# Decoder kernel on one core: the attention's values product moved behind the next step's scores, half of a copy given to GpSimd in the last block, and the first values products placed between the first scores

## The chip, the core and the metric

The kernel runs on one core of a Trainium2 chip. A core has five engines, each with its own instruction stream: TensorE (PE, matrix products; its weight loads are listed as PEld), VectorE (DVE), ScalarE (ACT), GpSimd (POOL) and SyncE (SP, which here only issues DMA transfers). They work from SBUF, the on-chip memory of 128 partitions; PE writes its results to PSUM, from which DVE and ACT read them. [...]

The metric is the time of one execution on the device in microseconds (us). A profiled execution of the same kernel, with a start and a length for each instruction, stands beside it.

## The reference

The input `x` has 8 sequences of 256 tokens with 256 features. Three parts follow one another, each with a residual and a layer norm:

```python
x = layernorm(x + attention(x))        # causal, 16 heads of 64
x = layernorm(x + cross_attention(x))  # 3 rounds against 120 context rows, each with a GRU cell
x = layernorm(x + ffn(x))              # shared MLP + best 2 of 8 experts
```

The change concerns the first part, and in a small place the beginning of the second:

```python
q, k, v = x @ Wq, x @ Wk, x @ Wv                       # 1024 columns: 16 heads of 64
logits = einsum('nhid,nhjd->nhij', q, k) / 8 + causal
out = einsum('nhij,nhjd->nhid', softmax(logits), v)
return out @ Wo + bo
```

All of it is computed in float32.

## The kernel before

The 2048 tokens are taken in four blocks of 512, which is two sequences each (`NBLK`, `BLK`, `BPB`). The attention runs in 64 steps; a step is one block `i`, one pair of heads `pr` and one sequence `bi` of the block, so there are 16 steps to a block. For a step:

- `scores` (L313) makes the products of queries and keys on PE for both heads, lower triangle only: for each head a 128x128 tile and a 128x256 tile, 384 columns together, in the PSUM tiles `pp` (a ring of three banks, two used by a step).
- `least` (L328) adds the mask on DVE and takes each row's minimum of the negated scores (four instructions with `nmax` as a second result); then ACT makes the exponentials in four instructions with their row sums, `sums`.
- `weigh` (L358) takes the reciprocal of the sums on DVE, and GpSimd multiplies the tile `sc` by it in two instructions.
- `split` (L370) separates the high and the low 16 bits of the float32 weights into `planes`: ACT copies all 1536 halves in one instruction. Then SP issues a DMA transpose of 16-bit words to `turned`.
- `joined` (L382) puts the two halves together again on DVE, which gives `pT`, the transposed weights.
- `attend_values` (L391) multiplies values by `pT` on PE, in `po`, and copies the result to `OT`: on ACT in blocks 0 to 2, on DVE in the last block.

`planes`, `turned`, `pT` and `po` have two buffers each, `sc` has four.

Beside the steps runs work of other blocks: `project` (L292) makes the queries or keys of the pair two or three ahead (PE, then a DVE copy `qk`); `values` (L303) makes an eighth of the next block's values; `outputs` (L415) multiplies a finished block by `Wo` and adds it to `X`; `to_feature_major` transposes a block on PE; `between` (L422) spreads these over the 16 steps of a block at fixed places (`V_AT`, `O_AT`), and near a block's end also takes the root for the layer norm (`root`, ACT and DVE) and scales the rows (`scaled`, DVE). `context_normed` puts small works of the second part into blocks 1 and 2, among them GpSimd products at L197.

In this part the order on PE, ACT, DVE and GpSimd is the order of the program text (`manual_schedule`, L257 and L262), so the driver loop (L485 to L501) is the schedule. The main loop takes step `k` to its end while step `k + 3` (`ahead` is 3) gets its scores and `k + 2` is weighed and split. SP's queue is in program order too: first the loads of the weights, then one transpose per step.

After the steps the remaining outputs are made, PSUM is taken over by new pools, and the second part begins with `context_transposed` (four groups of PE transposes, copied to `pnT` by DVE), `weights_joined` (two products `pa`, copied to `AT`, and two groups `pc`, copied to `C`) and `keys`, which needs both (L1003 to L1005). There DVE's and GpSimd's order comes from the planner; PE's and ACT's is still that of the text.

Of the kernel before, what the change touches and what calls it, by code (L numbers as in the profile page):

```python
# [12 lines left out]
U16 = mybir.dt.uint16  # L13
# [4 lines left out]
B, S, D = 8, 256, 256  # L18
# [7 lines left out]
NBLK = NT // BLK  # L26
NSUB = BLK // P
BPB = BLK // S
NPAIR = H // 2
# [32 lines left out]
def decoder_kernel(  # L62
# [23 lines left out]
    nc = tc.nc  # L86
# [14 lines left out]
    def evac(dst, src):  # L101

        flip[0] ^= 1
        if flip[0]:
            nc.vector.tensor_copy(dst, src)
        else:
            nc.scalar.copy(dst, src)
# [150 lines left out]
    with (  # L258
# [29 lines left out]
        OT = [None] * NBLK  # L288
# [3 lines left out]
        def project(g, which):  # L292

            i, pr = divmod(g, NPAIR)
            w = (wq_sb, wk_sb)[which]
            pq = bank(f"pq_{g}_{which}")
            for dc in range(DC):
                nc.tensor.matmul(pq, w[:, dc, ts(pr, P)], XT[i][:, dc, :], start=dc == 0, stop=dc == DC - 1)
            t = a4.tile([P, BLK], F32, tag=f"qk{which}", name=f"qk_{g}_{which}")
            nc.vector.tensor_copy(t, pq)  # L300
            qk[g, which] = t

        def values(i, n, hf):  # L303
            if V[i] is None:
                V[i] = a2.tile([P, NSUB, H * HD], F32, tag="v", name=f"v_{i}")
            pv = bank(f"pv_{i}_{n}_{hf}")
            for dc in range(DC):
                nc.tensor.matmul(
                    pv, XT[i][:, dc, ts(n, P)], wv_sb[:, dc, ts(hf, 512)], start=dc == 0, stop=dc == DC - 1
                )  # L310
            nc.vector.tensor_copy(V[i][:, n, ts(hf, 512)], pv)

        def scores(k):  # L313
            i, pr, bi = steps[k]
            g = i * NPAIR + pr
            qT, kT = qk[g, 0], qk[g, 1]
            t0 = bi * S
            pp = [ps_s.tile([P, 512], F32, tag="pp", name=f"pp_{k}_{h}") for h in range(2)]
            rows2 = [slice(h * HD, (h + 1) * HD) for h in range(2)]
            for h, r in enumerate(rows2):  # L320
                nc.tensor.matmul(pp[h][:, 0:P], qT[r, ds(t0, P)], kT[r, ds(t0, P)], start=True, stop=True)
            for h, r in enumerate(rows2):
                nc.tensor.matmul(pp[h][:, P:384], qT[r, ds(t0 + P, P)], kT[r, ds(t0, S)], start=True, stop=True)  # L323
            live[k] = pp
# [3 lines left out]
        def least(k):  # L328

            pp = live.pop(k)  # L330
            sc = a4.tile([P, 2, 384], F32, tag="sc", name=f"sc_{k}")
            nmax = stat.tile([P, 2, 2], F32, tag="nmax", name="nmax")
            for h in range(2):
                for t in range(2):
                    nc.vector.tensor_tensor_reduce(  # L335
                        out=sc[:, h, seg[t]],
                        in0=pp[h][:, seg[t]],
                        in1=mask[:, seg[t]],
                        scale=-(HD**-0.5),
                        scalar=3.0e38,  # L340
                        op0=ALU.add,
                        op1=ALU.min,
                        accum_out=nmax[:, t, h : h + 1],
                    )
            sums = stat.tile([P, 2, 2], F32, tag="sums", name="sums")
            for h in range(2):
                for t in range(2):
                    nc.scalar.activation(  # L348
                        sc[:, h, seg[t]],
                        sc[:, h, seg[t]],  # L350
                        AF.Exp,
                        scale=-1.0,
                        bias=nmax[:, t, h : h + 1],
                        accum_out=sums[:, t, h : h + 1],
                    )
            live[k] = sc, sums
# [13 lines left out]
        def split(k):  # L370

            sc, sums = live.pop(k)
            n = 2 * 384
            planes = a2.tile([P, 2, n], U16, tag="planes", name=f"planes_{k}")
            nc.scalar.copy(planes, sc.rearrange("p h c -> p (h c)").bitcast(U16).rearrange("p (n w) -> p w n", w=2))  # L377
            turned = a2.tile([P, 2 * n // P, P], U16, tag="turned", name=f"turned_{k}")
            nc.sync.dma_start_transpose(turned, planes.rearrange("p w n -> p (w n)"))
            live[k] = turned  # L380

        def joined(k):  # L382
            turned = live.pop(k)
            pT = a2.tile([P, 2, 384], F32, tag="pT", name=f"pT_{k}")
            nc.vector.tensor_copy(  # L385
                pT.rearrange("p h c -> p (h c)").bitcast(U16).rearrange("p (n w) -> p w n", w=2),
                turned.rearrange("p (w c) q -> p w (c q)", w=2),
            )
            live[k] = pT

        def attend_values(k):  # L391
            i, pr, bi = steps[k]
            pT = live.pop(k)
            if OT[i] is None:
                OT[i] = a2.tile([P, NPAIR, BLK], F32, tag="ot", name=f"ot_{i}")
            po = ps_o.tile([P, 512], F32, tag="po", name=f"po_{k}")[:, 0:S]
            for c, q0 in ((0, 0), (1, P)):
                for h in range(2):
                    nc.tensor.matmul(  # L399
                        po[ts(h, HD), q0:S],  # L400
                        V[i][:, 2 * bi + c, ts(2 * pr + h, HD)],
                        pT[:, h, 0:S] if c == 0 else pT[:, h, S:384],
                        start=c == 0,
                        stop=c == 1,
                    )
            if i + 1 < NBLK:
                nc.scalar.copy(OT[i][:, pr, ts(bi, S)], po)
            else:
                nc.vector.tensor_copy(OT[i][:, pr, ts(bi, S)], po)

        def add_bo(i):

# [2 lines left out]
        def outputs(i, n):  # L415
            py = bank(f"py_{i}_{n}")[:, 0:D]
            for pr in range(NPAIR):
                nc.tensor.matmul(py, OT[i][:, pr, ts(n, P)], wo_sb[:, pr, :], start=pr == 0, stop=pr == NPAIR - 1)
            nc.vector.tensor_tensor(X[i][:, n, :], py, X[i][:, n, :], ALU.add)
            MV[i] = moments(X[i], MV.get(i), (n,))  # L420
# [25 lines left out]
        ahead = 3  # L446
# [18 lines left out]
        add_bo(0)  # L465
        for which in range(2):
            project(0, which)
        for k in range(2):
            scores(k)
            least(k)  # L470
        weigh(0)
        values(0, 0, 0)
        split(0)
        values(0, 0, 1)
        weigh(1)
        split(1)
        for which in range(2):
            project(1, which)
        scores(2)
        least(2)  # L480
        for n in range(1, NSUB):
            for hf in range(2):
                values(0, n, hf)
        project(2, 0)
        for k in range(len(steps)):  # L485
            i, j = divmod(k, 2 * NPAIR)
            if k + ahead - 1 < len(steps):
                weigh(k + ahead - 1)
            if k + ahead < len(steps):
                scores(k + ahead)  # L490
                least(k + ahead)
            if k + ahead - 1 < len(steps):
                split(k + ahead - 1)
            joined(k)
            if k + 5 < 2 * NBLK * NPAIR:
                project(*divmod(k + 5, 2))
            elif k >= len(steps) - NSUB:

                outputs(NBLK - 2, k - len(steps) + NSUB)
            between(i, j)  # L500
            attend_values(k)  # L501
        normalize(X[NBLK - 2], MV[NBLK - 2])
        for n in range(NSUB):
            outputs(NBLK - 1, n)
# [118 lines left out]
                    ALU.mult,  # L623
                )

    def weights_joined():
        for d in range(DC):
            pa = bank(f"pa_{d}")
            for o in range(DC):
                nc.tensor.matmul(pa[:, 0:D], xwk_sb[:, o, ts(d, P)], xwq_sb[:, o, :], start=o == 0, stop=o == DC - 1)  # L630
            evac(AT[:, d, :], pa[:, 0:D])
        for d in range(DC):
            pc = big(f"pc_{d}")
            for hf in range(2):
                for o in range(DC):
                    nc.tensor.matmul(
                        pc[:, hf, 0:384],
                        xwv_sb[:, o, ts(d, P)],
                        wih_sb[:, o, ts(hf, 384)],
                        start=o == 0,  # L640
                        stop=o == DC - 1,
                    )
            evac(C[:, d, :].rearrange("p (a b) -> p a b", a=2), pc[:, :, 0:384])
# [352 lines left out]
    def both(*fs):  # L996
# [3 lines left out]

        return f

    context_transposed()  # L1003
    weights_joined()
    keys()  # L1005
    for p in range(2):
        norms(p)
# [265 lines left out]
    for a in range(half):  # L1273
        n = half + a
# [69 lines left out]
```

## Time and profile before

| | us |
|---|---|
| median of three runs (1064.96 to 1066.25) | 1065.13 |
| profiled execution | 1096.06 |
| its span, first to last instruction | 1094.4 |

The columns of the next table are stretches of the trace in us from its start, and busy us of each engine in that stretch.

| stretch | what runs | length | PE | DVE | ACT | POOL |
|---|---|---|---|---|---|---|
| 0 to 35.7 | loads, first projections and values | 35.7 | 32.3 | 13.3 | 10.3 | 6.9 |
| 35.7 to 112.4 | block 0 | 76.7 | 72.2 | 52.8 | 56.6 | 28.3 |
| 112.4 to 203.5 | block 1 | 91.1 | 88.3 | 59.0 | 63.0 | 31.9 |
| 203.5 to 288.4 | block 2 | 84.9 | 82.1 | 54.3 | 54.7 | 30.4 |
| 288.4 to 339.4 | block 3, steps with a projection | 51.0 | 44.5 | 39.5 | 39.4 | 19.4 |
| 339.4 to 376.4 | last steps and outputs | 37.0 | 34.5 | 18.8 | 8.9 | 6.9 |
| 376.4 to 736 | second part, shared MLP's first half, routing | 359.6 | 346.4 | 171.0 | 151.6 | 82.7 |
| 736 to 1094 | experts and end | 358.0 | 339.6 | 61.3 | 91.6 | 30.9 |

A busy PE is not a PE at its peak, since matmuls overlap and their ends are modelled; a gap in PE's row is a real gap, however. The granted TensorE clock is full but for five dips to half: at 198 us for 3.4 us, at 676 and 707 for 6.8 each, at 1041 for 17, and from 1092 on. The costliest groups of the attention steps by the page, with the number of instructions, total and mean: ACT's exponentials (L348) x256, 113.3 us, 444 ns; GpSimd's weighing (L363) x128, 105.4 us, 845 ns; ACT's `planes` (L377) x64, 93.2 us, 1457 ns; DVE's minima (L335) x256, 76.3 us, 354 ns; DVE's `pT` (L385) x64, 70.0 us, 1094 ns.

### The profile page before, as it was taken

The page shows a single profiled execution, that of the slowest core. Times are in us where ns is not written, and L with a number is a line of the kernel's source. Part 1 is how long each engine was busy: PE and PEld are TensorE (multiplying, and loading weights), DVE is VectorE, ACT ScalarE, POOL GpSimd, SP SyncE. Part 2 cuts the span into 40 slices and gives each one's busy share as a digit, 9 for nine tenths or more (in the row PEclk, how much of TensorE's full clock was granted, in tenths as well). Part 3 has the DMA queues.
Part 4 walks back from the last instruction along what each step waited for, and adds up shares of the span by engine and source line. Part 5 has one row for each costly group of instructions (what it writes and reads, how often), then busy time and mean ns, then how long its engine had stood idle before and what let it go on. Part 6 is the DMA issues. An engine that isn't in the chain of part 4 may idle for free. (4 is left out here: it accounts for less than half of the span.)

```text
span 1094.4 us, 13674 instructions
## 1 busy us (share of the span) xinstructions
PE 1039.8 (95%) x4686; PEld 720.9 (66%) x4686; DVE 470.0 (43%) x1394; ACT 476.0 (43%) x1140; POOL 237.3 (22%) x264
## 2 busy tenths in 40 slices
PE   8999999999888999999999999699999999999967
PEld 5444555555445755556565668588888888888756
DVE  3666666666776542434443687300011010110137
ACT  3567776666776024555555443122222222222213
POOL 2333422532234211221211023500000000000550
PEclk9999999999999999999999998999999999999969
DMA  9634433433344499940000011246675667663231
GB/s 325 107 76 84 86 65 67 73 73 71 74 87 94 153 348 348 349 140 0 1 1 1 0 40 39 78 155 219 205 249 204 232 203 248 215 211 111 82 97 62
DMA packets 195492, 144.24 MB, mean 132 GB/s; under 512 B 107551, under 2 KB 185951, under 8 KB 195423
## 3 DMA queue, kind: packets, MB, share of 16 engines
q1 hardware_dynamic: 191263, 132.88, 42.2%
q0 software_dynamic: 3072, 8.39, 2.4%
q10 hardware_dynamic: 1088, 2.10, 0.5%
q8 instruction: 37, 0.61, 0.2%
q14 instruction: 32, 0.26, 0.1%
HBM read 72.70 MB, written 45.48 MB: 108 GB/s over the span
## 5 line engine op out<-in xcount | busy, mean ns | idle before, releaser
L1053 ACT ACTIVATE hT_t<-ph_t,bt 128x256 f32<-128x256 f32 (+1 forms) x184 | 71.3, 438 | 202.6 <-issue 154.6
L363 POOL TENSOR_TENSOR sc<-sc,sums 128x256 f32<-128x256 f32 (+1 forms) x128 | 105.4, 845 | 212.5 <-DVE sums L360 212.5
L348 ACT ACTIVATE sc<-sc,nmax 128x128 f32<-128x128 f32 (+1 forms) x256 | 113.3, 444 | 72.5 <-DVE nmax L335 72.5
L1044 PE MATMUL ph_t<-xgT,w 128*128 128x256 f32 (+1 forms) x736 | 140.3, 348 | 0.8 <-ACT hT_t L1053 0.8
L1058 PE MATMUL pf_t<-w,hT_t 128*128 128x256 f32 x624 | 138.3, 379 | 0.0
L739 PE MATMUL gate<-XT,whh_sb 128*128 128x512 f32 x288 | 133.8, 593 | 0.0
L1044 PEld LDWEIGHTS ph_t<-xgT,w 128*128 128x128 f32 x736 | 123.8, 190 | 15.0 <-ACT hT_t L1053 1.0
L1058 PEld LDWEIGHTS pf_t<-w,hT_t 128*128 128x128 f32 x624 | 116.9, 190 | 15.0
L1172 POOL DMA_INDIRECT y<-yd,slot x32 | 30.9, 967 | 323.7 <-PE ph_s L1044 309.2
L335 DVE CUSTOM_DVE_ANT_0 sc<-pp,mask 128x128 f32<-128x128 f32 (+1 forms) x256 | 76.3, 354 | 52.3 <-PE pp L323 50.7
L377 ACT COPY planes<-sc 128x1536 uint16<-128x1536 uint16 x64 | 93.2, 1457 | 8.5 <-POOL sc L363 8.5
L739 PEld LDWEIGHTS gate<-XT,whh_sb 128*128 128x128 f32 x288 | 54.3, 190 | 48.5 <-issue 46.2
L1044 PE MATMUL ph_s<-XT,sh 128*128 128x256 f32 x256 | 66.6, 415 | 20.2 <-issue 19.3
L399 PEld LDWEIGHTS po<-pT,v 128*64 128x64 f32 x512 | 32.9, 136 | 68.1 <-issue 25.4
L1044 PEld LDWEIGHTS ph_s<-XT,sh 128*128 128x128 f32 x256 | 53.1, 210 | 32.1 <-issue 22.6
L748 PEld LDWEIGHTS gate<-at,G 120*128 120x128 f32 x288 | 54.5, 189 | 29.9 <-issue 23.3
L399 PE MATMUL po<-pT,v 128*64 128x256 f32 (+1 forms) x512 | 55.7, 337 | 19.1 <-DVE pT L385 15.0
L748 PE MATMUL gate<-at,G 120*128 120x256 f32 x288 | 72.1, 379 | 0.4 <-DVE at L598 0.4
L1149 DVE COPY xgT<-xg 128x512 f32<-128x512 f32 (+1 forms) x23 | 14.0, 611 | 131.8 <-PE xg L1147 131.8
L385 DVE COPY pT<-turned 128x1536 uint16<-128x1536 uint16 x64 | 70.0, 1094 | 0.0
L598 DVE TENSOR_TENSOR yo<-pf_t,b2t 128x512 f32<-128x512 f32 (+1 forms) x23 | 14.0, 610 | 127.9 <-PE pf_t L1058 127.9
L1053 ACT ACTIVATE hT_s<-ph_s,vec_sb 128x256 f32<-128x256 f32 x64 | 26.9, 471 | 90.5 <-PE ph_s L1044 44.6
(208 smaller groups left out, 1479.6 us busy)
## 6 DMA issues: line engine op xcount, KB each, us to landing
w<-in_ew_dram SPq DMA_DIRECT2D x46, 1024.0 KB, 5.5
xd<-zeros SPq DMA_DIRECT2D x1, 16640.0 KB, 51.3
yd<-zeros SPq DMA_DIRECT2D x1, 16640.0 KB, 99.4
xg<-xd SPq DMA_DIRECT2D x16, 256.0 KB, 5.3
yd<-yo SPq DMA_DIRECT2D x16, 256.0 KB, 5.6
b2t<-in_b_dram SPq DMA_DIRECT2D x23, 128.0 KB, 5.2
sh<-in_sh_w_dram SPq DMA_DIRECT2D x2, 1024.0 KB, 6.9
X<-in_x_dram SPq DMA_DIRECT2D x3, 512.0 KB, 11.7
```

Source lines behind the costliest of these rows:

```text
L335: nc.vector.tensor_tensor_reduce(out=sc[:, h, seg[t]], in0=pp[h][:, seg[t]], in1=mask[:, seg[t]], scale=-(HD**-0.5), scalar=3.0e38, op0=AL ...
L348: nc.scalar.activation(sc[:, h, seg[t]], sc[:, h, seg[t]], AF.Exp, scale=-1.0, bias=nmax[:, t, h : h + 1], accum_out=sums[:, t, h : h + 1],)
L363: nc.gpsimd.tensor_tensor(sc[:, :, seg[t]], sc[:, :, seg[t]], sums[:, t, :].unsqueeze(2).to_broadcast([P, 2, w]), ALU.mult,)
L377: nc.scalar.copy(planes, sc.rearrange("p h c -> p (h c)").bitcast(U16).rearrange("p (n w) -> p w n", w=2))
L385: nc.vector.tensor_copy(pT.rearrange("p h c -> p (h c)").bitcast(U16).rearrange("p (n w) -> p w n", w=2), turned.rearrange("p (w c) q -> p ...
L399: nc.tensor.matmul(po[ts(h, HD), q0:S], V[i][:, 2 * bi + c, ts(2 * pr + h, HD)], pT[:, h, 0:S] if c == 0 else pT[:, h, S:384], start=c == ...
L739: nc.tensor.matmul(pg[:, oc, :], whh_sb[:, dc, o], XT[i][:, dc, :], start=dc == 0, stop=not given and dc == DC - 1,)
L748: nc.tensor.matmul(pg[:, oc, ts(bi, S)], G[:, BPB * i + bi, o], AT_[p][:, bi, :], start=not hidden, stop=not hidden or bi == BPB - 1,)
L1044: nc.tensor.matmul(ph[:, a, 0:w], w1_sb[:, dc, ts(c, P)], rhs[:, dc, :], start=dc == 0, stop=dc == DC - 1,)
L1053: nc.scalar.activation(hT[:, c, 0:w], ph[:, a, 0:w], AF.Gelu_apprx_tanh, bias=bias[:, c : c + 1])
L1058: nc.tensor.matmul(po, hT[:, c, ts(a, P)], w2_sb[:, c, :], start=c == 0, stop=c == FC - 1)
L1172: nc.gpsimd.indirect_dma_start(out=y, out_offset=None, in_=yd[:, :], in_offset=bass.IndirectOffsetOnAxis(ap=slot[:, g : g + 1], axis=0),)
```

## The change

Four edits:

1. In the driver loop `attend_values` is called one turn later and at another place: for step `k - 1`, after the scores and minima of step `k + 3` and before `split`. The loop gets one more turn at its end. The last outputs of block 2 (`outputs(NBLK - 2, ...)`) go with it, in front of it, in the last four turns.
2. In the last block `split` gives the second head's half of `planes` to GpSimd and leaves the first head's half to ACT. The copy of `po` to `OT` is made by ACT in all blocks.
3. Before the loop the first three eighths of block 0's values are placed between the first projections and scores, and the projections of the second pair come before the second weighing.
4. The second part begins with the products `pa` (`attention_joined`), then the transposes of the context, then the products `pc` (`inputs_joined`).

```diff
@@ split
-            nc.scalar.copy(planes, sc.rearrange("p h c -> p (h c)").bitcast(U16).rearrange("p (n w) -> p w n", w=2))
+            words = sc.rearrange("p h c -> p (h c)").bitcast(U16).rearrange("p (n w) -> p w n", w=2)
+            if steps[k][0] + 1 < NBLK:
+                nc.scalar.copy(planes, words)
+            else:
+                nc.gpsimd.tensor_copy(planes[:, :, ts(1, n // 2)], words[:, :, ts(1, n // 2)])
+                nc.scalar.copy(planes[:, :, ts(0, n // 2)], words[:, :, ts(0, n // 2)])
@@ attend_values
-            if i + 1 < NBLK:
-                nc.scalar.copy(OT[i][:, pr, ts(bi, S)], po)
-            else:
-                nc.vector.tensor_copy(OT[i][:, pr, ts(bi, S)], po)
+            nc.scalar.copy(OT[i][:, pr, ts(bi, S)], po)
@@ before the loop
-        for k in range(2):
-            scores(k)
-            least(k)
+        values(0, 0, 0)
+        scores(0)
+        least(0)
+        values(0, 0, 1)
+        scores(1)
+        least(1)
         weigh(0)
-        values(0, 0, 0)
         split(0)
-        values(0, 0, 1)
+        for which in range(2):
+            project(1, which)
         weigh(1)
         split(1)
-        for which in range(2):
-            project(1, which)
+        values(0, 1, 0)
         scores(2)
         least(2)
-        for n in range(1, NSUB):
-            for hf in range(2):
-                values(0, n, hf)
+        for m in range(3, 2 * NSUB):
+            values(0, *divmod(m, 2))
         project(2, 0)
@@ the loop, as it is after the change
+        last = len(steps)
+        for k in range(last + 1):
+            i, j = divmod(k, 2 * NPAIR)
+            if k + ahead - 1 < last:
+                weigh(k + ahead - 1)
+            if k + ahead < last:
+                scores(k + ahead)
+                least(k + ahead)
+            if k:
+                if k > last - NSUB:
+                    outputs(NBLK - 2, k - 1 - last + NSUB)
+                attend_values(k - 1)
+            if k + ahead - 1 < last:
+                split(k + ahead - 1)
+            if k < last:
+                joined(k)
+                if k + 5 < 2 * NBLK * NPAIR:
+                    project(*divmod(k + 5, 2))
+                between(i, j)
@@ second part
+    attention_joined()
     context_transposed()
-    weights_joined()
+    inputs_joined()
     keys()
```

More of the change, by code (lines that the diff above doesn't have):

```diff
@@ L467, in decoder_kernel @@
             project(0, which)
-        for k in range(2):
-            scores(k)
-            least(k)
+        values(0, 0, 0)
[4 more added lines that the diff above has]
+        least(1)
         weigh(0)
-        values(0, 0, 0)
         split(0)
-        values(0, 0, 1)
+        for which in range(2):
+            project(1, which)
         weigh(1)
         split(1)
-        for which in range(2):
-            project(1, which)
+        values(0, 1, 0)
         scores(2)
         least(2)
-        for n in range(1, NSUB):
-            for hf in range(2):
-                values(0, n, hf)
+        for m in range(3, 2 * NSUB):
+            values(0, *divmod(m, 2))
         project(2, 0)
-        for k in range(len(steps)):
+        last = len(steps)
+        for k in range(last + 1):
             i, j = divmod(k, 2 * NPAIR)
-            if k + ahead - 1 < len(steps):
+            if k + ahead - 1 < last:
                 weigh(k + ahead - 1)
-            if k + ahead < len(steps):
+            if k + ahead < last:
                 scores(k + ahead)
                 least(k + ahead)
-            if k + ahead - 1 < len(steps):
-                split(k + ahead - 1)
[L494 to L501, printed above, removed]
+            if k:
[3 more added lines that the diff above has]
+            if k + ahead - 1 < last:
+                split(k + ahead - 1)
+            if k < last:
[3 more added lines that the diff above has]
+                between(i, j)
         normalize(X[NBLK - 2], MV[NBLK - 2])
@@ L624, in context_transposed, with attention_joined @@
                 )
-    def weights_joined():
+    def attention_joined():
         for d in range(DC):
@@ L631, in weights_joined, with inputs_joined @@
             evac(AT[:, d, :], pa[:, 0:D])
+    def inputs_joined():
         for d in range(DC):
```

## The prediction

> **What bounds the kernel now.** I read the slices first: PE is busy at 9 tenths or more almost throughout, and the chain that ended last is matmuls of the expert stage. So time that TensorE (PE) loses earlier is time of the kernel: whatever removes a PE wait in the attention stage (0 to 376 us of the trace) moves all that follows. Next, who PE waited for in 40 to 350 us (total, times, longest):
>
> ```profile
> engine line waited for: us in total, times, longest us
> PE po L399 <- DVE pT L385: 15.0, 15, 2.5
> PE po L399 <- ACT sc L348: 4.1, 8, 0.5
> ```
>
> Both rows are one place: `po`, the values product, waits for `pT`, the joined transpose. Then the timeline of one step of the last block (start, length, engine, idle before):
>
> ```profile
> 318.37 0.49 PE L321 MATMUL pp<-qk,qk 64*128 64x128 f32 x4
> 318.48 0.42 DVE L409 COPY ot<-po 128x256 f32<-128x256 f32 x1 [0.49 <-PE po L399]
> 318.82 0.17 DVE L360 RECIPROCAL sums<-sums 128x4 f32<-128x4 f32 x1
> 319.13 1.61 POOL L363 TENSOR_TENSOR sc<-sc,sums 128x256 f32<-128x256 f32 x2 [2.60 <-DVE sums L360]
> 319.23 1.98 PE L298 MATMUL pq<-XT,wk_sb 128*128 128x512 f32 x4
> 319.44 0.29 DVE L335 CUSTOM_DVE_ANT_0 sc<-pp,mask 128x128 f32<-128x128 f32 x1 [0.45 <-PE pp L323]
> 320.55 1.08 DVE L385 COPY pT<-turned 128x1536 uint16<-128x1536 uint16 x1
> 321.53 0.67 DVE L300 COPY qk<-pq 128x512 f32<-128x512 f32 x1
> 321.54 1.46 ACT L377 COPY planes<-sc 128x1536 uint16<-128x1536 uint16 x1
> 321.78 0.87 PE L399 MATMUL po<-pT,v 128*64 128x256 f32 x8 [0.57 <-DVE pT L385]
> 322.58 0.49 PE L321 MATMUL pp<-qk,qk 64*128 64x128 f32 x4
> ```
>
> It is a ring: scores (318.37), DVE's four minima behind them (319.44), `pT` behind those (320.55), values (321.78), next scores (322.58). A turn takes 4.21 us though no engine has that much work. PE's own share is scores 0.86 + projection 1.98 + values 0.80, less matmul tails: a step that also makes values of the next block takes 5.29 us without a wait, and those cost four 512-wide matmuls 0.43 apart, so PE's floor is 5.29 - 1.72 = **3.57 us**.
>
> From score start to score start: six plain steps of block 0 at 4.16; block 1's tail 4.63, 5.50, 6.09; block 2's tail 4.16, 5.96; last block 4.15, ten steps of 42.34 together, then 4.20 with no projection. Steps with values (5.29) or outputs (7.02) have no wait and gain nothing.
>
> **The values behind the next scores (about 16 of the gain).** The ring is cut: a step's values use the `pT` of the step before, so the minima and `pT` no longer stand between two PE groups. What is late next? Per plain step of blocks 0 to 2: ACT has exponentials 1.77 + `ot` 0.37 + `planes` 1.46 = 3.60, and `ot` now stands before `planes`, where it waits for nothing because the values follow the scores at once. Up to 0.1 us a step over PE's floor for two or three steps is absorbed: the exponentials are due only at the next step's reciprocal, 1.3 us later. DVE depends on a port it shares with GpSimd:
>
> ```profile
> 193.94 1.61 POOL L363 TENSOR_TENSOR sc<-sc,sums 128x256 f32<-128x256 f32 x2 [3.88 <-DVE sums L360]
> 194.78 1.67 DVE L385 COPY pT<-turned 128x1536 uint16<-128x1536 uint16 x1
> 195.51 1.37 POOL L197 TENSOR_TENSOR c_sb<-c_sb,cr 120x256 f32<-120x256 f32 x1
> ```
>
> `pT` takes 1.03 alone, but 1.67 when it starts inside GpSimd's product, and always ends 0.88 to 0.91 after the GpSimd instruction that held it. In the new order the product starts 0.31 after the reciprocal and runs 1.61, `pT` is asked for 1.23 after the reciprocal and so ends at 0.31 + 1.61 + 0.88 = 2.80; `qk` adds about 0.60 until the next reciprocal: 3.40 a step, 0.17 under PE's floor. The transpose (issue 1.43, landing 3.6 us after issue) is due two steps later: its data is ready some 4.8 us into a step, lands at 8.4, and is needed at 2 x 3.57 + 2.18 = 9.3.
> - Block 0: 6 x (4.16 - 3.57) = **3.5**.
> - First two steps: 9.47 now, of which 1.55 us is PE wait. Without values in step 0, PE now waits some 0.6 for `qk` behind a stretched `pT`, and 0.1 in step 1: **0.8**.
> - Block 1's tail: 16.22 us against 11.6 of PE work. DVE stays the limit there: the root's two ACT steps now follow `ot` and `planes`, its three small DVE steps and the scaling hold the next reciprocal to about 6.4 us after the last (6.0 now). That holds the second next scores 0.5 and the values 1.0: 1.6 of wait remains. 1.65 of the present loss is a half-speed clock for 3.4 us at 198, which may come again; half of it counted: **2.2**. Block 2's tail without that: 3.0 - 1.5 = **1.5**.
> - Tail: before, the step at 339.40 has nothing to fill 2.5 us. After, two steps lack a projection, but the second is followed at once by outputs: one wait until `pT`, about 1.3. **1.2**.
>
> **GpSimd takes half of `planes` in the last block (with `ot` moved back to ACT).** ACT: 1.77 + 0.37 + half of 1.46 with its fixed part, 0.84 = 2.98, not the limit. DVE loses `ot` (0.42). GpSimd gets a copy of 768 elements, which no row shows. Lower end: the Trainium skill, *GPSIMD Engine Reference*, "When to use GPSIMD", has one-input work at about line rate, 768 at 1.2 GHz plus 0.10 fixed (from 0.57 and 1.04 for 256 and 512 elements): an estimate of 0.75 us. Upper end: the two-input product's 1.8 ns an element, 1.5 us. The nearest row has one input: the 128-element selection at 1.17 us of the trace, 0.28, so 1.4 ns an element and **1.18 us**, which I take. A copy behind `pT` at the port finishes about 0.17 sooner after release than alone (the row at 195.51 ends 0.43 after `pT`, against 0.61). GpSimd's step is 1.61 + 0.88 + 1.18 - 0.17 + 0.1 of gaps = 3.6; by the page's rate 3.2 (PE's 3.57 stands), by the upper end 3.9. I take 3.65: 0.5 + (42.34 - 36.5) = **6.3**; the ends give 7.2 and 3.6.
>
> Here a rule speaks against the change: the skill's *SBUF — State Buffer*, "Who interferes with whom", says that a two-port DVE copy and GpSimd lock each other out for a whole instruction, whoever is first. The 0.88 us agrees. It decides by order: `pT` asks 0.7 us before the product ends, the half copy only at its end, so `pT` should be next, as at 194.78, where it went ahead of L197. By this the last block gains 6.3; were the copy first, see the second rival.
>
> **Values between the first scores (2.7).** PE is idle here before three score groups:
>
> ```profile
> 12.10 0.49 PE L321 MATMUL pp<-qk,qk 64*128 64x128 f32 x4 [0.78 <-DVE qk L300]
> 13.88 0.37 PE L321 MATMUL pp<-qk,qk 64*128 64x128 f32 x1 [0.64 <-DVE nmax L335]
> 22.65 0.49 PE L321 MATMUL pp<-qk,qk 64*128 64x128 f32 x4 [0.78 <-DVE qk L300]
> ```
>
> With values or projections in between, PE runs on: 0.95 + 0.80 + 0.95 = **2.7**. The first values need `wv_sb`: issued at 1.83, landed 8.8 later at 10.6; they would start at 11.2. The cover is 0.5 us, and lateness beyond it is paid one for one. The first weighing comes 1.9 later on DVE, but SP's queue was issuing loads until 21.9 before the first transpose anyway; the second transpose moves from 22.4 to about 24, due only at 38.
>
> **Stage two's weights first.** PE has 1.06 and 0.20 of idle before `pa` at 379.80 and 381.13. They go, but DVE now does the root and scaling before `pnT`, locked by GpSimd's squares, so `pnT` is ready at 387.2 instead of 383.5 and the keys wait a little: **0.5**.
>
> **Sum:** 3.5 + 0.8 + 2.2 + 1.5 + 1.2 + 6.3 + 2.7 + 0.5 = 18.7. The profiled execution's 1096.06 (span 1094.4) would become 1077. It is 31 us over the median, a difference I cannot place; stage waits are taken over unscaled: 1065.1 - 18.7 = **1046.4**.
>
> **Rivals.**
> 1. DVE limits the plain steps. Its ring of 3.40 is close to 3.57; another 0.35 of gaps or port waits makes 3.75 in about 18 plain steps: 18 x 0.2 = 3.6 less, **1050**; with the upper end of the copy 1053. For it: `pT` has been stretched by 0.3 to 0.6 wherever it met GpSimd. Against it: 3.40 already holds the full block.
> 2. The half copy takes the port before `pT`. The ring is then 0.31 + 1.61 + 1.18 + 0.88 + 0.60 = 4.6, 0.4 above today's: 11 x 0.37 lost, not 6.3 won: **1056.8**. For it: at 189.45 GpSimd's next instruction started with the earlier one's end and stayed in front of a `pT` that asked at that moment. Against it: 194.78, and the copy must wait for the product's result.
> 3. Slower: the half copy is far dearer, since it reads every second 16-bit word, which no row does. All else gains 12.4; eleven steps would have to lose more than 1.13 each, a step of 5.34 us, so from a copy of 2.9 us on. At 3.2 us, 5.62 a step: **1068.2**. Against it: twice the rate of a two-input product.
>
> **Chances.** Main case 0.66, rival 1 0.15, rival 2 0.14, rival 3 0.05. The main case's range is 1042.5 (the page's copy rate, no clock dip, 2 more in the tails) to 1049 (dip again, late `wv_sb`); rival 1 takes it to 1054, leaving out rivals 2 and 3. A change under 0.2% (2.1 us) cannot be told from none; that falls between rivals 2 and 3, 0.02. Faster 0.94, slower 0.04.
>
> **What would show it.** Right: `po` waits of PE almost gone outside the block tails; last-block steps near 3.6 us; scores of step 3 at 33 instead of 35.7 us; `pT` ending 0.9 after the product and before the half copy runs. Wrong: `pT` of 2 us or more in the last block, a half copy over 1.5 us, PE waiting for `wv_sb` at 11, or savings handed back as a wait in stage two.

## The result, and the profile after

| | before | after |
|---|---|---|
| median (lowest to highest), us | 1065.62 (1064.96 to 1066.25) | 1054.98 (1052.93 to 1057.97) |
| span of the profiled execution | 1094.4 | 1056.3 |

The ratio is 0.9902, with an interval of 0.9877 to 0.9928: faster by 10.6 us. The forecast was 18.7 us faster, 1046.4; its range ended at 1054, so the time lies just outside. The four times of the kernel after stand in the order of their mean granted TensorE clock, 0.998 for the lowest and 0.991 for the highest; the profiled one is the highest. The run with idle products, below, comes back to this.

The two spans must not be subtracted. A second profile of the unchanged kernel (run `before_again`: 1064.99 us, span 1063.3) has the same attention to within 0.02 us (last output product at 375.96 and 375.98), and the 31 us that the prediction could not place all lie behind it: 13.8 before the first expert product and 17.2 in the last part of the shared MLP. PE stood still for long there (busy for 21.3 of the 30 us from 690 to 720, and for 5.6 of the 17 from 1036 to 1053; in the second profile it has hardly a wait in the same work), and the half clock at 707 and 1041 falls within these stretches. Why PE stood there is open. So it is the attention that can be compared, up to the first product `pc` of the second part: it starts at 382.10 before and at 376.64 after, **5.5 us** earlier in this slowest execution.

From the page of the kernel after, its first part (busy us and share of each engine) and three of its costliest groups (count, busy us and mean ns, then idle time before):

```profile
PE 1031.2 (98%) x4686; PEld 714.5 (68%) x4686; DVE 484.3 (46%) x1378; ACT 466.6 (44%) x1156; POOL 257.4 (24%) x280
...
L391 DVE COPY pT<-turned 128x1536 uint16<-128x1536 uint16 x64 | 86.3, 1348 | 1.1 <-DMA turned<-planes 1.1
...
L379 ACT COPY planes<-sc 128x1536 uint16<-128x1536 uint16 x48 | 70.5, 1470 | 5.9 <-POOL sc L363 5.8
...
L405 PE MATMUL po<-pT,v 128*64 128x256 f32 (+1 forms) x512 | 57.1, 345 | 1.0 <-DVE sums L360 1.0
```

`po` (L405) waits 1.0 us in all, so the old wait for `pT` is gone, although `pT` is now slower (1348 ns against 1094): it takes over 1.2 us in 55 of 64 steps, against 7 before, 46 of the 55 starting inside GpSimd's product. Who PE waits for in the attention steps instead:

```profile
engine line waited for: us in total, times, longest us
PE pp L321 <- DVE qk L300: 13.3, 11, 2.9
PE po L405 <- DVE sums L360: 1.0, 1, 1.0
```

The two rows of before, 15.0 and 4.1, have given way to one of 13.3 at another place: the scores `pp` now wait for `qk`, DVE's copy of the projected keys. The timeline of two steps of the last block shows how (start, length, engine, idle before):

```profile
299.92 0.49 PE L321 MATMUL pp<-qk,qk 64*128 64x128 f32 x4
...
300.78 0.87 PE L405 MATMUL po<-pT,v 128*64 128x256 f32 x8
300.89 1.61 POOL L363 TENSOR_TENSOR sc<-sc,sums 128x256 f32<-128x256 f32 x2 [1.92 <-DVE sums L360]
...
301.58 1.98 PE L298 MATMUL pq<-XT,wk_sb 128*128 128x512 f32 x4
...
302.11 1.29 DVE L391 COPY pT<-turned 128x1536 uint16<-128x1536 uint16 x1
...
302.56 1.51 POOL L382 COPY planes<-sc 128x768 uint16<-128x768 uint16 x1
...
303.60 0.69 DVE L300 COPY qk<-pq 128x512 f32<-128x512 f32 x1 [0.21 <-PE pq L298]
...
304.35 0.49 PE L321 MATMUL pp<-qk,qk 64*128 64x128 f32 x4 [0.78 <-DVE qk L300]
...
306.13 0.82 POOL L382 COPY planes<-sc 128x768 uint16<-128x768 uint16 x1
...
306.53 1.31 DVE L391 COPY pT<-turned 128x1536 uint16<-128x1536 uint16 x1
...
307.92 0.49 PE L321 MATMUL pp<-qk,qk 64*128 64x128 f32 x4
...
308.03 0.69 DVE L300 COPY qk<-pq 128x512 f32<-128x512 f32 x1 [0.18 <-PE pq L298]
```

PE's last work of a turn is now the projection (301.58, `wk_sb`). In every second turn that makes the keys of the pair whose scores come first in the next turn. PE ends it, DVE copies it in 0.69, and only then can 304.35 start. Steps alternate: 4.43 us (299.92 to 304.35, with the wait at its end) and 3.57 (304.35 to 307.92, without). Before, the values stood between the projection and the scores, with their 0.80 us and the wait for `pT`; behind these the copy never showed.

In the tail of block 1 the same edge costs far more:

```profile
187.29 1.98 PE L298 MATMUL pq<-XT,wk_sb 128*128 128x512 f32 x4
...
187.51 0.16 DVE L232 SCALAR_TENSOR_TENSOR step<-mv,rstd 128x4 f32<-128x4 f32 x1 [0.96 <-ACT rstd L131]
...
188.10 0.74 DVE L239 TENSOR_SCALAR X<-X,mv,rstd 128x256 f32<-128x256 f32 x2
...
189.93 1.67 DVE L391 COPY pT<-turned 128x1536 uint16<-128x1536 uint16 x1
191.49 0.67 DVE L300 COPY qk<-pq 128x512 f32<-128x512 f32 x1
...
192.21 0.80 PE L321 MATMUL pp<-qk,qk 64*128 64x128 f32 x4 [2.94 <-DVE qk L300]
...
195.27 3.56 PE L298 MATMUL pq<-XT,wq_sb 128*128 128x512 f32 x4
```

The keys leave PE at 189.27, but their copy stands in DVE's queue behind the layer norm's root, the scaling and a `pT` that GpSimd stretches: it ends at 192.16 and PE has stood for 2.94 us. What follows is told by the last row, 3.56 us for a projection that takes 1.98. The stretches around it (busy us of each engine, granted clock PEclk, DMA):

```profile
core 0: us, PE busy (x) PEld busy (x) DVE busy (x) ACT busy (x) POOL busy (x), PEclk, DMA share, GB/s
...
187.00:189.00 2.00, 2.00 (x10) 0.79 (x6) 1.39 (x7) 0.45 (x3) 0.00 (x0) 1.00 0.43 82
192.20:195.00 2.80, 2.79 (x16) 1.70 (x16) 1.68 (x10) 1.09 (x4) 1.97 (x3) 0.50 0.45 86
195.20:199.00 3.80, 3.80 (x10) 1.74 (x9) 1.08 (x3) 2.63 (x8) 0.02 (x1) 0.57 0.16 29
199.00:203.00 4.00, 4.00 (x27) 2.30 (x26) 3.43 (x12) 2.55 (x10) 1.61 (x2) 1.00 0.52 98
```

The clock is at half for 6.8 us from 191.7 on. PE looks fully busy there; only the clock's column tells that it works at half speed.

What each part of the sum became, in us (the length of each part, from score start to score start, in the trace before less the same in the trace after; positive is gained):

| part | forecast | measured |
|---|---|---|
| start, to the scores of step 3 | 2.7 | 35.72 - 33.34 = 2.4 |
| first two steps | 0.8 | 9.47 - 8.44 = 1.0 |
| block 0, the rest | 3.5 | 67.24 - 65.44 = 1.8 |
| block 1 with its tail | 2.2 | 91.05 - 92.42 = -1.4 |
| block 2 with its tail | 1.5 | 89.41 - 92.29 = -2.9 |
| last block, steps with a projection | 6.3 | 46.51 - 44.40 = 2.1 |
| last steps and outputs | 1.2 | 36.56 - 35.95 = 0.6 |
| last output to the first `pc` | 0.5 | 6.14 - 4.36 = 1.8 |

### The profile page after: what moved, and what is told of

Same layout as the page of the kernel before. It is cut to its first block, busy times and chain, and to the rows that moved or that the text cites. A ratio compares the mean times of both kernels' runs of the same rounds, so it can differ in the third digit from the quotient of the medians.

```text
span 1056.3 us, 13679 instructions
## 1 busy us (share of the span) xinstructions
PE 1031.2 (98%) x4686; PEld 714.5 (68%) x4686; DVE 484.3 (46%) x1378; ACT 466.6 (44%) x1156; POOL 257.4 (24%) x280
## 5 line engine op out<-in xcount | busy, mean ns | idle before, releaser
L391 DVE COPY pT<-turned 128x1536 uint16<-128x1536 uint16 x64 | 86.3, 1348 | 1.1 <-DMA turned<-planes 1.1
L379 ACT COPY planes<-sc 128x1536 uint16<-128x1536 uint16 x48 | 70.5, 1470 | 5.9 <-POOL sc L363 5.8
L298 PE MATMUL pq<-XT,wq_sb 128*128 128x512 f32 x128 | 66.4, 643 | 0.0
L298 PE MATMUL pq<-XT,wk_sb 128*128 128x512 f32 x128 | 63.3, 617 | 0.0
L308 PE MATMUL pv<-wv_sb,XT 128*128 128x512 f32 x128 | 59.7, 594 | 0.0
L405 PE MATMUL po<-pT,v 128*64 128x256 f32 (+1 forms) x512 | 57.1, 345 | 1.0 <-DVE sums L360 1.0
L421 PE MATMUL py<-wo_sb,ot 128*128 128x256 f32 x256 | 57.9, 381 | 0.0
```

The source lines that it names most:

```text
L308: nc.tensor.matmul(pv, XT[i][:, dc, ts(n, P)], wv_sb[:, dc, ts(hf, 512)], start=dc == 0, stop=dc == DC - 1)
L379: nc.scalar.copy(planes, words)
L391: nc.vector.tensor_copy(pT.rearrange("p h c -> p (h c)").bitcast(U16).rearrange("p (n w) -> p w n", w=2), turned.rearrange("p (w c) q -> p ...
```

## The experiments

Two theories stood after the result. **A**: what is left is the new edge, from the projection over DVE's copy to the scores. **B**: DVE and its shared port limit the steps (rival 1), and the wait for `qk` is only where that shows. Ratios are to the kernel before on the same chip.

### Each projection one turn earlier (`ahead6`)

```diff
         project(2, 0)
+        project(2, 1)
@@ the loop
-                if k + 5 < 2 * NBLK * NPAIR:
-                    project(*divmod(k + 5, 2))
+                if k + 6 < 2 * NBLK * NPAIR:
+                    project(*divmod(k + 6, 2))
```

The keys get a whole turn between PE and the scores; DVE's, ACT's and GpSimd's work per turn stays the same.

> The changed kernel, with each projection made one turn earlier (before the loop queries and keys of pair 2, in the loop k + 6 instead of k + 5). Theory A (the new wait is the scores of a new pair for DVE's copy qk of keys projected just before them): the waits of PE pp for DVE qk, 13.3 us in 11 times, go except in the two block tails; every plain step of the last block takes 3.6 us instead of 3.57 and 4.42 in turn, so five times 0.85 there, 1.7 in block 0 and 1.2 in the first steps: about 7 us less than the changed kernel, 1048. Theory B (DVE's ring through the port shared with GpSimd sets the pace): the wait moves to po for pT, plain steps stay at about 4.0 on average, and the time stays near 1055.

1042.41 us, ratio 0.9782 (0.9763 to 0.98): 12.6 less than the kernel after. Its waits in the attention steps, and a plain step:

```profile
engine line waited for: us in total, times, longest us
PE po L405 <- DVE pT L391: 3.0, 3, 1.3
PE po L405 <- ACT ot L412: 0.9, 1, 0.9
```

```profile
285.75 0.49 PE L321 MATMUL pp<-qk,qk 64*128 64x128 f32 x4
...
286.06 0.67 DVE L300 COPY qk<-pq 128x512 f32<-128x512 f32 x1
...
286.60 0.87 PE L405 MATMUL po<-pT,v 128*64 128x256 f32 x8
...
286.66 0.16 DVE L360 RECIPROCAL sums<-sums 128x4 f32<-128x4 f32 x1
...
287.40 1.98 PE L298 MATMUL pq<-XT,wk_sb 128*128 128x512 f32 x4
...
289.32 0.49 PE L321 MATMUL pp<-qk,qk 64*128 64x128 f32 x4
...
290.04 0.17 DVE L360 RECIPROCAL sums<-sums 128x4 f32<-128x4 f32 x1
...
290.38 0.29 DVE L335 CUSTOM_DVE_ANT_0 sc<-pp,mask 128x128 f32<-128x128 f32 x1 [0.18 <-PE pp L323]
```

There is no row for `qk`; the copy (286.06) now runs beside the scores of the step before, and every plain step takes 3.57 us (285.75 to 289.32; the first alone 3.64), the floor of the prediction. B would have kept steps above that. DVE still makes a full turn, from reciprocal to reciprocal, in 3.38 us without idle (286.66 to 290.04), and then waits for PE (290.38). The two block tails take 13.27 us from their first plain step on, and there is no half clock in the whole attention. A holds. The gain is more than the 7 us of the expectation because that left the tails' waits standing: by the traces blocks 1 and 2, each with its tail, go from 92.4 and 92.3 us to 88.1.

### The values behind the projection (`values_last`)

```diff
@@ the loop
-            if k:
-                if k > last - NSUB:
-                    outputs(NBLK - 2, k - 1 - last + NSUB)
-                attend_values(k - 1)
             if k + ahead - 1 < last:
                 split(k + ahead - 1)
...
                 between(i, j)
+            if k:
+                if k > last - NSUB:
+                    outputs(NBLK - 2, k - 1 - last + NSUB)
+                attend_values(k - 1)
```

The values of step `k - 1`, still without the ring, stand again between the projection and the scores.

> The changed kernel with the values of step k - 1 at the end of turn k, behind the projection, instead of directly behind the scores. Theory A: the values (0.80 us of PE) stand between the keys' projection and the scores that need their copy, so of the 0.95 us wait 0.15 stays; plain steps of the last block 3.6 to 3.7, total about 6 us less than the changed kernel, 1049. Theory B: no change, about 1055.

1050.04 us, ratio 0.9845 (0.9826 to 0.9864). The wait is there but smaller, in as many places, and plain steps alternate between 3.84 and 3.57:

```profile
PE pp L321 <- DVE qk L300: 7.7, 11, 2.6
```

So 0.80 us of other PE work hides most of the edge: a step is 0.27 longer than the floor instead of 0.85, and in the tails the wait is still 2.6. (The expectations count a wait some 0.16 longer than this view does: 0.95 for its 0.78, 3.1 for its 2.94.)

### The first edit undone (`old_place`)

```diff
@@ the loop
-            if k:
-                if k > last - NSUB:
-                    outputs(NBLK - 2, k - 1 - last + NSUB)
-                attend_values(k - 1)
...
             if k + ahead - 1 < last:
                 split(k + ahead - 1)
             joined(k)
             if k + 5 < 2 * NBLK * NPAIR:
                 project(*divmod(k + 5, 2))
+            elif k >= last - NSUB:
+                outputs(NBLK - 2, k - last + NSUB)
             between(i, j)
+            attend_values(k)
```

> The changed kernel with the values of step k back in turn k at its end, so only the first order, the split copy and the second part's start are changed. If the move of the values brought what the changed kernel gained in the plain steps, this has steps of 4.16 to 4.2 in block 0 again; in the last block the ring without DVE's copy of po is the values 0.80, scores 0.86, minima 1.1, pT 1.1 and two hand-overs, 4.2. Block tails 15.2 us instead of 17.6 without half-speed clock. Both theories expect about 1062 (2.7 from the start and 1 from the second part less than before), and A expects no wait of pp for qk.

1061.56 us, ratio 0.9958 (0.9942 to 0.9974). Plain steps are at 4.15 to 4.16 again, and PE waits where it did before the change, though partly for another engine by the records:

```profile
PE po L405 <- ACT sc L348: 11.2, 18, 2.4
PE po L405 <- DVE pT L391: 4.7, 5, 1.8
PE po L405 <- ACT planes L383: 2.3, 1, 2.3
```

So the moved values are worth 6.6 us, and all else some 4 to 4.6, about what the start (2.4) and the beginning of the second part (1.8) show. In the last block the half copy and `ot` on ACT bring a step from 4.21 to 4.16 only.

### ACT copies all of `planes` (`whole_copy`, and `ahead6_whole` on top of `ahead6`)

```diff
-            if steps[k][0] + 1 < NBLK:
+            if True:
                 nc.scalar.copy(planes, words)
```

> The changed kernel with the whole of planes copied by ACT in the last block too. ACT has 1.77 + 0.35 + 1.47 = 3.6 us a step there. Theory A: the pair of steps still takes 8.0 because it is set by the wait for qk, so the time is the changed kernel's within 1 us. Theory B (port): GpSimd's half copy no longer stands in front of anything, pT shortens and the last block gains 2 us or more.

> The changed kernel with projections one turn earlier and with the whole of planes copied by ACT in the last block. ACT then has 1.77 + 0.35 + 1.47 = 3.6 us a step against 3.57 of PE: steps of 3.6, so at most 0.5 us more over the last block than with the half copy, 1042 to 1043. If the half copy is what makes room for 3.57, the steps go to 3.8 or more and the time to 1045 or more.

1054.87 us (0.9889, 0.9869 to 0.991), with the same 4.42 and 3.57; and 1043.72 us (0.9806, 0.9782 to 0.9831), again with 3.57 in every plain step. In the trace of `ahead6_whole`, `pc` starts 0.27 us later than in `ahead6`. The half copy brings nothing that can be measured, with the edge or without it.

### The projections ahead, without the moved values (`before_ahead6`)

The same edit as in `ahead6`, on the kernel before.

> The kernel before with each projection made one turn earlier and nothing else. Theory A says that an earlier projection is worth something only where the scores follow a projection directly; here the values stand between, and the ring scores, minima, pT, values sets the step: no change, 1066, plain steps still 4.16. If instead the projection's place alone brought the 12.6 us that the changed kernel gained by it, this would be near 1053.

1068.89 us, ratio 1.0042 (1.0027 to 1.0057): slower, where no change was expected. Plain steps stay at 4.16, for there the ring through `pT` decides, and the additional projection in front of the loop is not won back (`pc` 1.3 us later in the trace; another 1.7 lies behind the attention, where the dip at 677 lasts 6.8 us instead of 3.4). Each of the two edits removes one of two edges that lie beside each other: from `old_place` to the kernel after, the moved values bring 6.6 us; with the projections ahead as well (`ahead6`) it is 19.1.

### Idle products in the tails (`after_filled`, with `after_again` beside it)

Did the half clock come from PE's standing still? The first fills the wait of 2.94 us with ten products of ones whose result nothing uses; the second is the kernel after once more.

```diff
                 weigh(k + ahead - 1)
+            if j == 2 * NPAIR - 1 and i in (1, 2):
+                fill = bank(f"fill_{k}")
+                for _ in range(10):
+                    nc.tensor.matmul(fill[:, 0:P], ones, ones, start=True, stop=True)
             if k + ahead < last:
```

> The changed kernel, unchanged, for more executions with their granted clocks. In its first profile TensorE's clock was halved for 6.8 us in each of the two block tails, behind waits of 3.1 us, and the tails took 3 us more for it. If that comes and goes, executions spread by 5 us (1053 to 1058) in step with the clock, and a profile without the dips shows block 1 and block 2 at 89.4 us from first score to first score. If the dips were fixed to the waits, all executions would lie within 2 us.

> The changed kernel with ten idle 128x128 products on PE, about 2.2 us, ahead of the scores in the last turn of blocks 1 and 2, where PE waits 3.1 us. They fit into the wait, so by themselves they cost nothing. If the half-speed clock comes from PE standing idle, the two dips in the tails do not appear and the time is 1053, at the lower end of the changed kernel's. If the clock follows something else, or PE's load, the dips stay or get longer and it is 1055 to 1058.

These ran on a chip where the kernel before takes 1100.52 us: all kernels were some 35 us longer there, in the same two stretches behind the attention as in the first profile of before. `after_again` takes 1091.93 us (ratio 0.9918, 0.9901 to 0.9934) and `after_filled` 1088.9 (0.9893, 0.9877 to 0.991), so 3.0 less. With the filling no half clock is granted in either tail (the products, recorded as twenty, the scores behind them, and the stretches after these with PEclk):

```profile
188.74 2.39 PE L497 MATMUL fill<-ones 128*128 128x128 f32 x20
191.85 0.49 PE L321 MATMUL pp<-qk,qk 64*128 64x128 f32 x4 [0.72 <-DVE qk L300]
...
192.00:195.00 3.00, 3.00 (x20) 1.64 (x21) 2.61 (x12) 2.02 (x9) 2.33 (x3) 1.00 0.56 106
195.00:199.00 4.00, 4.00 (x29) 2.42 (x28) 3.19 (x13) 3.53 (x12) 2.22 (x3) 1.00 0.38 72
```

The last two steps of the first tail take 6.59 and 4.44 us instead of 6.58 and 7.42, the scores start no earlier, and `pc` starts at 370.46 instead of 376.22. Each dip thus costs **2.9 us**, and standing still brings it on.

The profiled executions of the kernel after and of `after_again`, and of `whole_copy`, all have both dips. Two dips less would be 5.8 us; the spread of the kernel after, 5.0 us, has about this size and goes with the granted clock. That some executions have fewer of these dips was not seen in a trace, but the mean clocks say so: 0.998 over 1051 us leaves an estimated 4 us at half speed, about what the dip at the end takes by itself in the profiled execution (4.5), while both dips of the tails would add 13.7. So the fastest execution cannot have had them.

### The root's ACT steps earlier in the tails (`ahead6_root`)

What `ahead6` still waits for in a tail is `pT`, behind the root and the scaling. Here the two ACT steps of the root (`first_root`, taken out of `root`) go in front of `planes` in the tails, so that DVE's small steps need not wait for ACT.

```diff
...
+            if k < last and 0 < i < NBLK - 1 and j == O_AT[-1] + 1:
+                RS[i - 1] = first_root(X[i - 1], MV[i - 1])
             if k + ahead - 1 < last:
                 split(k + ahead - 1)
```

> The changed kernel with projections one turn earlier, and with the two ACT steps of the layer norm's root put before planes in the block tails instead of behind it. DVE then gets the root 1.47 us earlier and no longer waits 1 us for it, so the PE wait of 1.47 us at po in the last step of blocks 1 and 2 falls to about 0.5: 2 us less in all, 1040.5. If the tails are held by DVE's own work (scaling, two stretched pT) rather than by its wait for ACT, it stays at 1042.

1041.14 us, ratio 0.9788 (0.9766 to 0.9809). The longest step of a tail goes from 6.12 to 5.07 us, PE's wait in it from 1.31 to 0.56, and `pc` starts 2.5 us earlier. This is the lowest time of all, and the wait has fallen about as expected, but its ratio cannot be told from that of `ahead6`.

### The second part's old order (`ahead6_context`)

```diff
-    attention_joined()
     context_transposed()
+    attention_joined()
     inputs_joined()
```

> The changed kernel with projections one turn earlier and the second part's start as before (context transposes first, then pa). From the last output product to the first product pc the kernel before takes 6.1 us and the changed one 4.4. If that is the order of the second part alone, this takes 6.1 again and 1.8 us more than without it, 1044.2. If part of it came from elsewhere (DVE's normalizing, which stands at another place), less than 1 us is lost.

1078.82 us, ratio 0.9804 (0.9788 to 0.9821; `ahead6` has 0.9782, and the intervals overlap). The expectation missed: from the last output to `pc` it takes 4.35 us, as with the new order (4.37). The fourth edit is not what gained 1.8 us there. Before:

```profile
376.68 1.90 POOL L685 TENSOR_TENSOR sq<-XT 128x1024 f32<-128x1024 f32 x1
376.72 1.87 DVE L606 TENSOR_TENSOR brz<-vec_sb 128x4 f32<-128x4 f32 x1
```

and in this run, with the same order of PE's work:

```profile
356.32 0.15 DVE L614 TENSOR_TENSOR brz<-vec_sb 128x4 f32<-128x4 f32 x1
356.33 1.91 POOL L695 TENSOR_TENSOR sq<-XT 128x1024 f32<-128x1024 f32 x1
```

A sum of 4 elements takes 0.15 us when it is 0.01 ahead of GpSimd's squares, and 1.87 when it is 0.04 behind them; what DVE does next for PE stands behind it. The difference of 1.72 is about the gain of 1.8. All three profiles of `before`, `before_again` and `before_ahead6` have the late form, and all eleven others the early one. That this order makes the difference is read from the rows; no run changed it alone. Which edit moves the two by 0.05 us was not tried.

### Block 2's last outputs earlier (`ahead6_outputs`)

On top of `ahead6_root`, `outputs(NBLK - 2, ...)` two turns earlier, behind the values, to fill the last steps without a projection.

> The changed kernel with projections one turn earlier and the root's ACT steps ahead of planes, and with block 2's last outputs in turns 58 to 61, where the projections have run out, instead of 61 to 64. PE's two waits for pT there, 1.08 and 0.57 us, are then filled, and nothing else changes: 1.6 us less, 1039.5. If DVE falls behind by the 1.03 us that it adds to each of these turns, a wait of that size comes back at po and it stays at 1041.

1088.59 us, ratio 0.9894 (0.9878 to 0.9911): slower than `ahead6_root` (0.9788) instead of faster. The last output product ends 14 us later in the trace than in `ahead6_root`, and PE waits for `pT` and the sums:

```profile
PE po L411 <- DVE pT L397: 8.7, 4, 5.4
PE po L411 <- DVE sums L366: 4.9, 3, 2.2
```

In that turn the outputs stand in front of `joined`. DVE's addition to `X` waits for the outputs' products with `pT` queued behind it, and the next values wait for `pT`: a new ring. The longest of the waits, 5.4, ends with a `pT` that has itself waited 5.2 us for its transpose.

## Why the prediction was wrong, point by point

- **The step that failed** is "The ring is cut: a step's values use the `pT` of the step before ... What is late next?" The prediction asked ACT, DVE's port and the transpose, and found all three in time, which they are. It did not ask what the scores themselves need. Every second score group needs the `qk` of the projection that PE ends directly before it. The sum had this wait in one place, "some 0.6 for `qk`" in the first two steps, but laid it to a stretched `pT` and put it at nothing in the plain steps. It costs 0.85 us in every second plain step, where block 0 and the last block lost 1.7 and 4.2 us of the forecast. `ahead6` takes this edge alone away and reaches 3.57 everywhere.
- **The tails** were forecast with 1.6 us of wait left and half a dip. The same edge made one wait of 2.94 in each and a dip of twice the length: 3.6 and 4.4 us short of the forecast. Of this 2.9 in each are the dip (`after_filled`). With the edge gone, the first tail takes 13.27 us, where the sum had 14.0.
- **PE's floor of 3.57** and the DVE ring of 3.40 were right: in `ahead6` the steps take the first, and DVE's turn without idle takes 3.38. Rival 1 falls, though its 1050 is nearer to the time than the main case: plain steps did stay above PE's floor, but for the moment at which DVE gets to one copy, not for the length of its turn.
- **The port's order** was right in half of the steps. In the timeline above, `pT` asks at 302.11 and ends at 303.40, 0.90 after the product; the half copy (302.56) is held until then. But in every second step, where the scores have waited for `qk` and the minima come late, the half copy goes first (306.13) and `pT` follows (306.53), which is the order of rival 2: 8 of the 16 copies. It costs PE nothing there, for DVE still waits for PE's next projection behind it (308.03). Rival 2 falls as a cause: without the half copy the steps are as long (`whole_copy`), and without the edge `pT` goes first in all plain steps of the last block (`ahead6`). So its 1056.8, the nearest of all, is near by chance: a time alone doesn't tell the mechanism. Both orders fit the rule of the Trainium skill that was weighed (*SBUF — State Buffer*, "Who interferes with whom"): the one that comes first holds the port, the other waits.
- **The half copy** takes 0.82 us when nothing holds it (306.13), near the estimate from the page's rate (the Trainium skill, *GPSIMD Engine Reference*, "When to use GPSIMD": 0.75) and not near the row I chose (1.18). Rival 3 falls. But the size did not matter: the last block's 6.3 was put down to this edit, and `ahead6_whole` has the same steps without it. By the prediction's own sum for blocks 0 to 2, ACT's 3.60 with the whole copy was already within 0.03 of PE's floor; the last block should have been costed by the same sum.
- **Values between the first scores**: 2.4 for 2.7. Right; PE did not wait for `wv_sb`. The idle in the three rows shown is 2.2; the 2.7 counts each some 0.16 longer.
- **The first two steps**: 1.0 for 0.8, but the wait for `qk` in them was 1.16, not 0.6, so the figure is no proof of its reasons.
- **Second part**: 1.8 for 0.5, for a cause that the prediction did not have.
- **The range** was built from the known costs' bounds. The case "another edge of the same ring" was not in it, and that is what came.

## What to carry to other kernels

When a group is moved out from between two others on an engine, list what the later of these needs from the one now directly before it: the work that was moved had also hidden that edge. A wait of a few us on PE can cost as much again, if the clock falls in it (here 2.94, and 2.9 more for the dip); so a rare long wait is worth removing before several short ones. And two edits that each remove one of two parallel edges must be priced together: here one alone was worth 6.6 us, the other alone, on the kernel before, made it slower, and together they brought 19, the vanished dips included.

## What the runs showed of the hardware

- After a PE wait of 2.94 us the granted clock was at half for 6.8 us in all six tails profiled of `after`, `after_again` and `whole_copy`. After waits of 1.85 to 2.6 us (before, `old_place`, `values_last`) it came in some places and not in others; after those of up to 1.3 us (`ahead6`) never. The Trainium skill, *TensorE: Matmul & The Clock Gate*, "HAM oscillation — how this bites in real kernels", gives as abstract rule that gaps over about 3.4 us are to be avoided; here shorter ones sufficed.
- The traces show what decides. In each of them all half-clock stretches start whole multiples of 3.413 us apart (after: 191.65 and 283.81, 27 of them), and those that do not run into the trace's end last 3.4 us or a multiple. Cut the attention of all 14 traces at these marks, and look at the pieces that run at full clock: in 13 of them PE stood still for 1.85 us or more, and a half clock followed each; in the other 1351 it stood for 1.73 or less, and none followed. So a wait counts by how much of it falls between two marks, and one of 2 us may pass or not. The half clock then went on for a second piece where PE stood for 0.56 us or more in its first (7 times), and ended where it stood for 0.29 or less (6 times). Behind the attention this does not suffice: the first half clock there (at 653 to 677 us) began with 1.6 us of standing or less in every trace that has one, in some with none.
- A copy of 768 16-bit elements that takes every second word costs GpSimd 0.82 us; held at the port, it ends 0.67 us after `pT` lets it go.
- In all 14 profiles the order in which one small DVE sum and GpSimd's squares began, 0.05 us apart, went with 1.7 us of DVE's time (0.15 or 1.87).
